# Mamba stages of a fused kernel: one batch and 1024 tokens a step, one scan per 1024 columns, sums over states for two groups at once

## The chip, the cores and the metric

The kernel runs on one core of one Trainium2 chip. The metric is the device time of one execution in microseconds, as the median of several runs; lower is better. The engines are TensorE (PE, matmuls; PEld is its weight load), VectorE (DVE), ScalarE (ACT), GpSimd (POOL) and SyncE (SP, which here issues the DMAs). All run their own instructions in order and wait for each other by semaphores.

## What is computed

Four layers in a row on an image batch of 4 x 96 channels x 64 x 64: a Mamba fusion block, an SSD block, a second Mamba fusion block and a ConvNeXt block. The change touches the two fusion blocks alone, which are the same code with other weights. All is float32. With L = 64 x 64 = 4096 tokens, DIN = 192 inner channels and 16 states per channel, one fusion is, cut to what matters:

```python
seq = x.reshape(b, c, L).transpose(0, 2, 1)
for i in range(2):                                   # two Mamba layers
    h = layernorm(seq); xs, z = split(h @ in_w, 2)
    xc = silu(causal_conv(xs, 4 taps) + conv_b)
    dt, Bm, Cm = split(xc @ xproj_w)                 # 6, 16, 16 columns
    delta = softplus(dt @ dt_w + dt_b)
    dA  = exp(delta[..., None] * A)                  # (b, L, 192, 16)
    dBx = delta[..., None] * Bm[:, :, None, :] * xc[..., None]
    hstates = linear recurrence over L: h[t] = dA[t] * h[t-1] + dBx[t]
    y = einsum('blds,bls->bld', hstates, Cm) + Dp * xc
    seq = seq + (y * silu(z)) @ out_w
gp = relu(x.mean((2, 3)) @ gp_w.T + gp_b)            # pooled branch, per batch
out = fus_w @ concat([mamba_out, broadcast(gp)])     # then batch norm, + x
```

The costly part is the recurrence: 4 batches x 4096 tokens x 192 channels x 16 states, twice per fusion, four times in the kernel.

## The kernel before

**Tiling.** `mamba_fusion` handles the batches in two pairs. `X` (L560) holds both batches of a pair in on-chip memory, channels on partitions. A *step* is one pair, one layer (`sub`) and T = 512 tokens; there are 2 x 2 x 8 = 32 steps per fusion (L623), 64 in the kernel. The 192 channels of two batches make 384 rows, that is three tiles j = 0, 1, 2 of 128 partitions; `SEGS` and `ROWS` (L49 to L55) say which rows of a tile are which channels of which batch: tile 0 is batch 0, tile 2 is batch 1, tile 1 is 64 rows of each.

**Groups.** For the recurrence each partition holds one channel and one state: 8 channels x 16 states fill 128 partitions. A *group* is two such sets (GS = 2), 128 partitions x 2 x 512 columns. A step has 24 groups: j (3) by q (4 blocks of 8 channels in a block of 32) by half p (2), counted in this order. The two sets of a group are quarters p and p + 2 of a tile, so they are different channels, and for j = 1 of different batches; hence they have different decay factors, and for j = 1 different rows of B and C (`b_or_c`, L328).

**One step's front.** `mamba_front` (L159) makes what the groups of a step need: layer norm (L174 to L196), four convolution taps as matmuls into `pu` (L205), silu, the gate rows `pz` (L215), the B, C and step-size rows `pd` (L228), softplus (L283 to L299), then `delta` and `delta * xc` (L251, L252) which are stored to DRAM (L246). B and C rows are stored and read back broadcast (L262). It is a generator: each `next` issues one piece. `PACE` (L279) says how many pieces are issued in each of the 24 iterations, so the front of the next step lies between the groups of this one.

**The run loop** (`Scan.run`, L458) has one iteration per group. In iteration n it issues, in this order: `load` for group n+5 (two DMAs that read 8 rows of delta and broadcast them to 16 states); `spread` for n+1 (TensorE copies delta * xc to the states, L343, into one of two `bs` buffers; for one group in four, the *dma* groups, the spread comes by DMA and `bs` holds the decays instead); `decay` for n+2 (ScalarE exponentials, L357); `after` for n-1 (GpSimd multiplies the scanned states with C into one of four `hc` buffers, L383; ScalarE copies the last column to `carry`, L386); `product` for n+2 (GpSimd, dma groups, L351); `scan` for n (VectorE: product with B, L369, if not a dma group; the gate product `close` of an earlier j, L410; then two scans of 512 columns, L376); the copies of finished output (`keep`, `spread_out`, `reload`); pieces of the front; `sums` for n-3 (TensorE sums over the states into `py`, L402, and adds D * xc, L396); and the output projection (L418 to L426) into `po`. A dependency written out by hand (L497 to L502) keeps this order on every engine. So the order of issue is also the order in which each engine works; an instruction that waits holds back all behind it on its engine.

**Around it.** Before the loop, front(0) runs by itself, and between its pieces the sums of `x` over all tokens for the pooled branch are made (L636 to L647): batches 0 and 1 from `X`, batches 2 and 3 from eight extra loads. `other_weights` (L650) loads the second layer's weights and folds the fusion matrix into them within the first steps. After the last group, statistics for the batch norm are put together (L687).

The two scans of a group are:

```python
for i in range(GS):
    n = NQU * g["quarters"][i] + g["q"]
    init = 0.0 if c == 0 else self.carry[:, j, n : n + 1]
    nc.vector.tensor_tensor_scan(hs[:, i], da[:, i], dbx[:, i], init, ALU.mult, ALU.add)
```

## Time and profile before

| what | value |
|---|---|
| median of the 3 runs | 9624.49 us (9616.18 to 9635.07) |
| span of the profiled execution | 9613.6 us |
| mean granted TensorE clock | 0.938 of full speed |
| busy share PE / DVE / ACT / POOL | 86% / 84% / 58% / 71% |
| scans L376, all forms | 3072 of 128x512 |
| products with C on POOL, L383 | 1536 of 128x1024, mean 2358 ns |
| sums on PE, L402 | 6144 records of 128x512 with 32 columns, mean 633 ns |
| spreads on PE, L343 | 4608 records, mean 682 ns |
| decays on ACT, L111 | 2304 + 768 of 128x512, means 710 and 688 ns |
| first fusion, SSD, second fusion, ConvNeXt begin at | 0, 2969, about 6069 and 9028 us |

How to read it: the profile lists instructions by source line, engine and operation, with the shape of the output and the inputs, the count, the busy time, the mean duration of one, and the idle time of the engine right before it with what ended it. A float32 matmul is recorded as two instructions. Records of neighbouring instructions on one engine can overlap by some tens of nanoseconds, so distances between starts say more than durations. In the timeline each line has start, duration, engine, source line, operation, tiles and a count where several of a kind follow each other. A bracket gives the idle time before and its releaser.

### The profile page before, as it was taken

How to read it: one execution, taken by the hardware profiler on the slowest of the kernel's cores; microseconds unless marked ns; L12 is line 12 of the kernel's file. 1: busy time of each engine (PE TensorE's matmuls, PEld its weight loads, DVE VectorE, ACT ScalarE, POOL GpSimd, SP SyncE). 2: the span in 40 equal slices, each digit the busy share in tenths (PEclk: the TensorE clock that was granted, in tenths of full speed). 3: DMA queues.
4: the chain of work that ended last, by engine and by line, in shares of the span. 5: the costliest groups of instructions: out<-in, count | busy, mean ns of one | idle time of the engine just before them, and what ended most of it. 6: DMA issues, size and time to landing. Idle time of an engine off the chain costs nothing. (4 is left out here: it accounts for less than half of the span.)

```text
span 9613.6 us, 109902 instructions
## 1 busy us (share of the span) xinstructions
PE 8280.0 (86%) x32896; PEld 3476.0 (36%) x32896; DVE 8048.5 (84%) x10870; ACT 5532.2 (58%) x10786; POOL 6872.2 (71%) x4573
## 2 busy tenths in 40 slices
PE   8888888888887998988898899788888888888678
PEld 2222222222213676776776767222222222222122
DVE  8999999999995666666767667799999999999887
ACT  5666666666664455445545544566666666666345
POOL 7888888888884555555555555688888988888511
PEclk8999999999997999999999999899999999999889
DMA  8788888777884223222322322687888877887643
GB/s 214 194 209 214 207 219 211 203 208 205 213 217 117 69 73 90 73 68 81 89 64 77 88 68 63 161 206 198 213 215 213 222 207 199 214 216 205 172 115 84
DMA packets 813856, 1531.93 MB, mean 159 GB/s; under 512 B 126894, under 2 KB 132426, under 8 KB 809803
## 3 DMA queue, kind: packets, MB, share of 16 engines
q1 hardware_dynamic: 810186, 1519.79, 60.5%
q8 instruction: 260, 4.26, 0.2%
q10 hardware_dynamic: 3072, 5.11, 0.1%
q14 instruction: 338, 2.76, 0.1%
HBM read 1229.28 MB, written 148.50 MB: 143 GB/s over the span
## 5 line engine op out<-in xcount | busy, mean ns | idle before, releaser
L383 POOL TENSOR_TENSOR hc<-hs,bc 128x1024 f32<-128x1024 f32 x1536 | 3613.9, 2358 | 671.8 <-DVE hs L376 427.8
L376 DVE TENSOR_TENSOR_SCAN hs<-da,carry,bs 128x512 f32<-128x512 f32 x2016 | 2468.7, 1266 | 98.9 <-ACT bs L111 2.0
L343 PE MATMUL bs<-du,seldu 64*128 64x512 f32 x4608 | 1488.7, 682 | 683.3 <-DVE hs L376 676.8
L402 PE MATMUL py<-hc,selsum 128*32 128x512 f32 x6144 | 1619.3, 633 | 34.4 <-DVE xz L410 28.9
L111 ACT ACTIVATE da<-da,w_a 128x512 f32<-128x512 f32 x2304 | 1518.3, 710 | 9.4 <-DMA da<-dd 9.2
L369 DVE TENSOR_TENSOR bs<-bs,bc 128x1024 f32<-128x1024 f32 x1152 | 1396.9, 1213 | 47.8 <-PE bs L343 37.3
L343 PEld LDWEIGHTS bs<-du,seldu 64*128 64x128 f32 x4608 | 409.0, 196 | 1687.9 <-DVE hs L376 1272.5
L351 POOL TENSOR_TENSOR du<-du,bc 128x1024 f32<-128x1024 f32 x384 | 905.5, 2358 | 17.9 <-DMA du<-dg 9.5
L111 ACT ACTIVATE bs<-da,w_a 128x512 f32<-128x512 f32 x768 | 528.6, 688 | 670.9 <-DVE hs L376 657.3
L1055 DVE TENSOR_SCALAR seg<-dr,dac 128x128 f32<-128x128 f32 x1536 | 636.5, 448 | 281.3 <-PE y L1100 278.7
L1071 POOL TENSOR_TENSOR seg<-seg,cb 128x384 f32<-128x384 f32 x512 | 515.2, 1008 | 480.9 <-DVE cb L1070 405.0
L376 DVE TENSOR_TENSOR_SCAN hs<-bs,carry,du 128x512 f32<-128x512 f32 x672 | 818.8, 1259 | 0.0
L205 PE MATMUL pu<-h,w_conv 96*128 96x512 f32 (+3 forms) x2048 | 794.2, 622 | 1.4 <-POOL h L179 1.4
L1006 PE MATMUL front<-pk,sconv 128*128 128x512 f32 x1536 | 755.2, 609 | 26.7 <-ACT z L994 21.6
L1110 POOL TENSOR_TENSOR y<-y,xs 128x192 f32<-128x192 f32 x496 | 295.9, 597 | 598.0 <-DVE y L1109 581.9
L1123 ACT ACTIVATE y<-yz 128x192 f32<-128x192 f32 x512 | 186.1, 364 | 901.7 <-DVE yz L1122 900.9
L402 PEld LDWEIGHTS py<-hc,selsum 128*32 128x32 f32 x6144 | 217.8, 110 | 1252.5 <-issue 781.2
L1075 POOL TENSOR_TENSOR xs<-pre,coef 128x576 f32<-128x576 f32 x512 | 599.0, 1175 | 51.8 <-ACT pre L116 25.1
L1017 PE MATMUL front<-sconv,pk 128*128 128x192 f32 x3072 | 571.8, 329 | 56.1 <-DVE pre L1022 50.8
L386 ACT COPY carry<-hs 128x2 f32<-128x2 f32 x1344 | 246.8, 184 | 530.6 <-DVE hs L376 530.1
L1017 PEld LDWEIGHTS front<-sconv,pk 128*128 128x128 f32 x3072 | 496.3, 190 | 88.4 <-DVE pre L1022 77.4
L1100 PEld LDWEIGHTS y<-xs,seg 128*128 128x128 f32 x3072 | 440.2, 205 | 141.4 <-issue 80.9
(229 smaller groups left out, 13717.5 us busy)
## 6 DMA issues: line engine op xcount, KB each, us to landing
da<-dd SPq DMA_DIRECT2D x3072, 256.0 KB
du<-dg SPq DMA_DIRECT2D x768, 256.0 KB
dr<-rows SPq DMA_DIRECT2D x256, 384.0 KB
bc<-rows SPq DMA_DIRECT2D x256, 256.0 KB
dd<-delta SPq DMA_DIRECT2D x192, 256.0 KB
dg<-du SPq DMA_DIRECT2D x192, 256.0 KB
pk<-xn SPq DMA_DIRECT2D x128, 384.0 KB
pk<-xn SPq DMA_DIRECT2D x128, 256.0 KB
```

The costliest lines, as they stand in the source:

```text
L111: self.last = self.scalar.activation(out, in_, func, **kw)
L205: nc.tensor.matmul(pu[r0:r1], lhsT=wt["conv"][:kk, tap, d0:d1], rhs=h[:kk, b, ds(tap, T)], start=(tap == 0), stop=(tap == 3),)
L343: nc.tensor.matmul(g["bs"][:, i], lhsT=self.sel["du"][rows, g["half"], g["q"]], rhs=g["made"]["du"][rows, g["j"]], start=True, stop=True,)
L351: self.tc.nc.gpsimd.tensor_tensor(g["du"], g["du"], self.b_or_c(g, 0), ALU.mult)
L369: nc.vector.tensor_tensor(dbx, dbx, self.b_or_c(g, 0), ALU.mult)
L376: nc.vector.tensor_tensor_scan(hs[:, i], da[:, i], dbx[:, i], init, ALU.mult, ALU.add)
L383: nc.gpsimd.tensor_tensor(g["hc"], hs, self.b_or_c(g, 1), ALU.mult)
L402: nc.tensor.matmul(py[rows], lhsT=self.sel["sum"][:, g["q"]], rhs=g["hc"][:, i], start=(g["q"] == 0), stop=(g["q"] == NQU - 1),)
L1006: nc.tensor.matmul(p, lhsT=self.conv[:, i, DI + q * DST : DI + (q + 1) * DST], rhs=pk[:, i, ds(c * T, T)], start=(i == 0), stop=(i == 2),)
L1017: nc.tensor.matmul(p, lhsT=pk[:, i, ds(c * Q, Q)], rhs=self.conv[:, i, :DI], start=(i == 0), stop=(i == 2),)
L1055: nc.vector.tensor_scalar(seg[:, h], g["pair"]["dr"][:, c % 2 * NH + h], made["dac"][:, n0 + h : n0 + h + 1], 0.0, ALU.subtract, ALU.min,)
L1075: nc.gpsimd.tensor_tensor(xs, x.to_broadcast([P, 3, NH, HD]), coef.to_broadcast([P, 3, NH, HD]), ALU.mult)
```

## The change

A step is now one batch, one layer and 1024 tokens (`STEP`). There are again 32 steps per fusion. The lower 64 partitions of every tile hold the first 512 tokens, the upper 64 the next 512, for the same 64 channels (`D0`: tile 0 has channels 0 to 63, tile 1 128 to 191, tile 2 64 to 127). So:

- The two sets of a group are the same 8 channels at neighbouring stretches of time. One scan of 1024 columns goes through both, with one start value and one carry column; one exponential of 1024 columns makes their decays, since the factor is the same; B and C are one plain tile for each group.
- In the front, every matmul over channels becomes two with 64 columns each (one per half of the tokens); the B, C and step-size weights stand on both halves of the partitions, and each half of the rows is multiplied by itself.
- `sums` is called for every second group and issues the four matmuls of two groups (halves p = 0 and 1, which go to four blocks of 32 rows of `py`) behind each other, at lag 3 and 4. The D product comes in the same call.
- The output projection of both token halves follows the last gate of the step (`completed`, lags 4 to 9) instead of one batch after j = 1 and one after j = 2; each has four matmuls. `PACE` is changed, with two iterations without a piece of the front.
- The sums of `x` for the pooled branch are made by ScalarE in the front of layer 0 (a copy with an accumulated sum); the extra loads and reductions before the loop go. The pooled branch is computed per batch (`pooled_rows`), the second layer's weights later, in `later`, a list of generators with starting iterations.
- At the start only batch 0 is loaded; batch 1 follows behind front(0).
- A step with c = 0 starts its scans from 0.0: one step in 4 instead of one in 8.

The core of the diff:

```diff
-SEGS = (
-    ((0, 128, 0, 128, 0),),
-    ((0, 64, 128, 192, 0), (64, 128, 0, 64, 1)),
-    ((0, 128, 64, 192, 1),),
-)
-ROWS = (((0, 0, 128), (1, 0, 64)), ((1, 64, 128), (2, 0, 128)))
+STEP = 2 * T
+NS = L // STEP
+D0 = (0, 128, 64)
...
+            xs = X[:, at, ds(c * STEP + n * T, T)]
             pc = bank("pc")[:C]
-            nc.tensor.matmul(
-                pc, lhsT=k.center, rhs=X[:, n, ds(c * T, T)], start=True, stop=True
-            )
+            nc.tensor.matmul(pc, lhsT=k.center, rhs=xs, start=True, stop=True)
             sq = work.tile([P, T], F32, tag="ua", name="sq", bufs=2)[:C]
+            if parts is not None:
+                nc.scalar.activation(sq, xs, AF.Copy, accum_out=parts[:, 2 * c + n : 2 * c + n + 1])
             nc.scalar.activation(sq, pc, AF.Square)
...
-            for r0, r1, d0, d1, b in SEGS[j]:
+            for i in range(2):
                 nc.tensor.matmul(
-                    pu[r0:r1], lhsT=wt["conv"][:kk, tap, d0:d1], rhs=h[:kk, b, ds(tap, T)],
-                    start=(tap == 0), stop=(tap == 3),
+                    pu[HALFP * i : HALFP * (i + 1)],
+                    lhsT=wt["conv"][:kk, tap, D0[j] : D0[j] + HALFP],
+                    rhs=h[:kk, ds(i * T + tap, T)], start=(tap == 0), stop=(tap == 3),
...
-    for n in range(2):
-        for b in range(2):
-            j, r0, r1 = ROWS[b][n if b == 0 else 1 - n]
+    for j in range(3):
+        for i in range(2):
+            half = ds(HALFP * i, HALFP)
             nc.tensor.matmul(
-                pd[2 * QUART * b : 2 * QUART * (b + 1)], lhsT=wt["xproj"][r0:r1, j],
-                rhs=xz[r0:r1, j], start=(n == 0), stop=(n == 1),
+                pd[half], lhsT=wt["xproj"][half, j], rhs=xz[half, j], start=(j == 0), stop=(j == 2),
...
-PACE = (1,) * 6 + (2, 2, 1, 1) + (2, 1) * 3 + (1,) * 8
+PACE = (1,) * 6 + (2, 0, 2, 2, 0, 2, 2, 2, 1, 1, 1, 2) + (1,) * 6
...
-        if g["j"] == 1:
-            return bc[:, :, which]
-        return bc[:, g["j"] // 2, which : which + 1].to_broadcast([P, GS, T])
+        return g["made"]["bc"][:, which]
...
-        for i in range(GS):
-            n = NQU * g["quarters"][i] + g["q"]
-            self.k.act.exp_ln(
-                out[:, i], g["da"][:, i], AF.Exp, scale=g["wt"]["a"][:, g["j"], n : n + 1]
-            )
+        n = g["n"]
+        self.k.act.exp_ln(out, g["da"], AF.Exp, scale=g["wt"]["a"][:, g["j"], n : n + 1])
...
-        for i in range(GS):
-            n = NQU * g["quarters"][i] + g["q"]
-            init = 0.0 if c == 0 else self.carry[:, j, n : n + 1]
-            nc.vector.tensor_tensor_scan(hs[:, i], da[:, i], dbx[:, i], init, ALU.mult, ALU.add)
+        n = g["n"]
+        init = 0.0 if c == 0 else self.carry[:, j, n : n + 1]
+        out, da, dbx = (x.rearrange("p i t -> p (i t)") for x in (hs, da, dbx))
+        nc.vector.tensor_tensor_scan(out, da, dbx, init, ALU.mult, ALU.add)
...
-        if g["c"] < NT - 1:
-            n = NQU * g["quarters"][0] + g["q"]
-            nc.scalar.copy(self.carry[:, g["j"], n : n + 2 * NQU + 1 : 2 * NQU], hs[:, :, T - 1])
-    def sums(self, g):
+        if g["c"] < NS - 1:
+            n = g["n"]
+            nc.scalar.copy(self.carry[:, g["j"], n : n + 1], hs[:, 1, T - 1 : T])
+    def sums(self, g, other):
         nc = self.tc.nc
-        if g["first"]:
-            g["made"]["py"] = self.psum.tile([P, T], F32, tag="py", name="py", bufs=1)
-        py = g["made"]["py"]
-        if g["q"] == NQU - 1 and g["half"] == 0:
-            nc.tensor.matmul(
-                py, lhsT=g["wt"]["d"][:, g["j"]], rhs=g["made"]["xz"][:, g["j"]], start=False,
-                stop=False,
-            )
-        for i in range(GS):
-            rows = ds(QUART * g["quarters"][i], QUART)
-            nc.tensor.matmul(
-                py[rows], lhsT=self.sel["sum"][:, g["q"]], rhs=g["hc"][:, i],
-                start=(g["q"] == 0), stop=(g["q"] == NQU - 1),
-            )
+        q, j, made = g["q"], g["j"], g["made"]
+        if q == 0:
+            made["py"] = self.psum.tile([P, T], F32, tag="py", name="py", bufs=1)
+        py = made["py"]
+        if q == NQU - 1:
+            nc.tensor.matmul(py, lhsT=g["wt"]["d"][:, j], rhs=made["xz"][:, j], start=False, stop=False)
+        for x in (other, g):
+            for i in range(GS):
+                nc.tensor.matmul(
+                    py[ds(HALFP * i + QUART * x["half"], QUART)], lhsT=self.sel["sum"][:, q],
+                    rhs=x["hc"][:, i], start=(q == 0), stop=(q == NQU - 1),
...
+    def project(self, g, i, part):
         nc = self.tc.nc
-        xz, wt = g["made"]["xz"], g["wt"]
-        po = self.po = self.psum.tile([P, T], F32, tag="po", name="po", bufs=1)[:C]
-        xs = self.X[:, b, ds(g["c"] * T, T)]
-        nc.tensor.matmul(po, lhsT=wt["of_x"], rhs=xs, start=True, stop=False)
-        j, r0, r1 = ROWS[b][0]
-        nc.tensor.matmul(
-            po, lhsT=wt["out"][r0:r1, j], rhs=xz[r0:r1, j], start=False, stop=False
-        )
-    def project_rest(self, g, b):
-        j, r0, r1 = ROWS[b][1]
-        self.tc.nc.tensor.matmul(
-            self.po, lhsT=g["wt"]["out"][r0:r1, j], rhs=g["made"]["xz"][r0:r1, j], start=False,
-            stop=True,
-        )
-    def keep(self, g, b):
-        xs = self.X[:, b, ds(g["c"] * T, T)]
+        if part == 0:
+            self.po = self.psum.tile([P, T], F32, tag="po", name="po", bufs=1)[:C]
+            nc.tensor.matmul(
+                self.po, lhsT=g["wt"]["of_x"], rhs=self.tokens(g, i), start=True, stop=False
+            )
+        half = ds(HALFP * i, HALFP)
+        for j in (2,) if part else (0, 1):
+            nc.tensor.matmul(
+                self.po, lhsT=g["wt"]["out"][half, j], rhs=g["made"]["xz"][half, j], start=False,
+                stop=(j == 2),
+            )
...
+                b=b, sub=sub, c=c, wt=wts[sub], made=made[n], j=j, q=q, half=p, n=NQU * p + q,
+                last=(q == NQU - 1 and p == 1), dma=(q % 2 == 0 and p == 1),
+            )
+            for n, (b, sub, c) in enumerate(steps) for j, q, p in units
...
+            completed(
+                (6, self.keep, 0, (0, 1)), (7, self.spread_out, 0, (1,)), (8, self.reload, 0, (1,)),
+                (9, self.keep, 1, (0, 1)), (10, self.spread_out, 1, (1,)), (11, self.reload, 1, (1,)),
...
-            if n in range(each, each + 14) or n in range(2 * each + 8, 2 * each + 12):
-                next(later, None)
-            if g := at(3):
-                self.sums(g)
-            completed((5, self.project, (0, 1)), (6, self.project_rest, (0, 1)))
+            if later and n >= later[0][0]:
+                if next(later[0][1], True):
+                    later.pop(0)
+            if (g := at(3)) and g["half"]:
+                self.sums(g, at(4))
+            completed(
+                (4, self.project, 0, (0, 1), 0), (5, self.project, 0, (0, 1), 1),
+                (7, self.project, 1, (0, 1), 0), (8, self.project, 1, (0, 1), 1),
...
-    carry = one.tile([P, 3, P // HEIGHT], F32, name="carry")
-    steps = [(pair, sub, c) for pair in range(B // 2) for sub in range(2) for c in range(NT)]
+    carry = one.tile([P, 3, HALFP // HEIGHT], F32, name="carry")
+    steps = [(b, sub, c) for b in range(B) for sub in range(2) for c in range(NS)]
+    parts = one.tile([C, B, NT], F32, name="parts")
...
-    for n, _ in enumerate(front(0, made)):
-        if n in (7, 11):
-            b = n // 4 - 1
-            nc.vector.reduce_sum(gsum[:, b : b + 1], X[:, b], axis=AX.X)
-        if n in (13, 15, 17, 19):
-            for m in range(n - 13, n - 11):
-                b, c = 2 + m // (L // BLK), m % (L // BLK)
-                x = state.tile([P, GS, T], F32, tag="da", name="x", bufs=8)[:C]
-                nc.sync.dma_start(
-                    x, src[b, :, ds(c * BLK, BLK)].rearrange("c (i t) -> c i t", i=GS)
-                )
-                nc.vector.reduce_sum(parts[:, b, c : c + 1], x.rearrange("c i t -> c (i t)"), axis=AX.X)
-    nc.vector.reduce_sum(gsum[:, 2:], parts[:, 2:], axis=AX.X)
-    gb = one.tile([C, B], F32, name="gb")
+    for _ in front(0, made):
+        pass
+    nc.sync.dma_start(X[:, 1], src[1])
...
+    def pooled_rows(b):
+        at = slice(b, b + 1)
+        nc.vector.reduce_sum(gsum[:, at], parts[:, b], axis=AX.X)
+        yield
+        pg = psum.tile([P, T], F32, tag="po", name="pg", bufs=1)[:C, :1]
+        nc.tensor.matmul(pg, lhsT=gpw, rhs=gsum[:, at], start=True, stop=True)
+        nc.scalar.activation(gp[:, at], pg, AF.Relu, bias=vec[:, 0:1], scale=1.0 / L)
+        yield
+        pg = psum.tile([P, T], F32, tag="po", name="pg", bufs=1)[:C, :1]
+        nc.tensor.matmul(pg, lhsT=fus[:, 1], rhs=gp[:, at], start=True, stop=True)
+        nc.scalar.activation(gb[:, at], pg, AF.Identity, bias=vec[:, 1:2])
+    each = 3 * HALFP // HEIGHT
+    later = [(each, other_weights()), (2 * each + 9, folded())] + [
+        ((2 * b * NS + NS - 1) * each + 9, pooled_rows(b)) for b in range(B)
```

## The prediction

> **What bounds the kernel now.** I read the shares by slice first, then the two Mamba stages apart from the rest, then VectorE's groups, its waits, and stretches of the timeline.

> ```profile
> DVE  8999999999995666666767667799999999999887
> POOL 7888888888884555555555555688888988888511
> DMA  8788888777884223222322322687888877887643
> ```

> VectorE is full in slices 1 to 12 and 26 to 37 and in no others: these are the two Mamba fusions, the only code that the change touches. SSD and ConvNeXt between and behind them stay as they are. A steady window inside the first fusion (us, then the busy time of PE, PEld, DVE, ACT, POOL, the granted clock, the DMA share and GB/s):

> ```profile
> 600.00:2700.00 2100.00, 1828.89 (x5791) 434.57 (x5788) 1972.99 (x1787) 1335.70 (x2484) 1830.23 (x881) 0.95 0.81 210
> ```

> VectorE is busy for 94% of it, TensorE and GpSimd for 87%, ScalarE for 64%, the DMA engines for 81%. So VectorE sets the pace, with two engines close behind. 557 of the 1536 groups (a group is one pass of the run loop, 1024 columns) lie in this window, 3.77 us each; a step of 24 groups takes 90.5 us, the window is 23.2 steps, and the kernel has 64 of them. VectorE's main groups in the window and everything that it waited for by name:

> ```profile
> L376 DVE TENSOR_TENSOR_SCAN hs<-da,carry,bs 128x512 f32<-128x512 f32 x726 | 889.0, 1266 | 35.2 <-ACT bs L111 0.5
> L369 DVE TENSOR_TENSOR bs<-bs,bc 128x1024 f32<-128x1024 f32 x417 | 506.0, 1213 | 11.4 <-PE bs L343 6.9
> L376 DVE TENSOR_TENSOR_SCAN hs<-da,bs 128x512 f32<-128x512 f32 x108 | 125.8, 1206 | 5.5 <-ACT bs L111 0.5
> L410 DVE TENSOR_TENSOR xz<-py,xz 128x512 f32<-128x512 f32 x69 | 47.4, 687 | 66.6 <-PE py L402 66.6
> ```

> The reader is to see that the scans are over 60% of VectorE's time, and that its one real wait is the gate product at L410 for TensorE's sums: 66.6 us, with 6.9 us at L369 makes 73.5 us, or 3.2 us a step.

> **Scans, two of 512 columns into one of 1024.** Mean durations overlap, so I price by distances between starts.

> ```profile
> 1590.65 1.21 DVE L369 TENSOR_TENSOR bs<-bs,bc 128x1024 f32<-128x1024 f32 x1
> 1591.76 0.68 DVE L410 TENSOR_TENSOR xz<-py,xz 128x512 f32<-128x512 f32 x1
> 1592.36 2.32 DVE L376 TENSOR_TENSOR_SCAN hs<-da,bs 128x512 f32<-128x512 f32 x2
> ...
> 1598.18 2.31 DVE L376 TENSOR_TENSOR_SCAN hs<-bs,du 128x512 f32<-128x512 f32 x2
> 1600.41 1.21 DVE L369 TENSOR_TENSOR bs<-bs,bc 128x1024 f32<-128x1024 f32 x1
> 1601.72 2.33 DVE L376 TENSOR_TENSOR_SCAN hs<-da,bs 128x512 f32<-128x512 f32 x2
> 1603.97 1.21 DVE L369 TENSOR_TENSOR bs<-bs,bc 128x1024 f32<-128x1024 f32 x1
> ...
> 1611.27 0.66 DVE L178 TENSOR_TENSOR h<-pc,rs 96x512 f32<-96x512 f32 x1
> 1611.85 2.44 DVE L376 TENSOR_TENSOR_SCAN hs<-bs,carry,du 128x512 f32<-128x512 f32 x2
> ...
> 1624.54 2.45 DVE L376 TENSOR_TENSOR_SCAN hs<-da,carry,bs 128x512 f32<-128x512 f32 x2
> 1626.90 2.43 DVE L376 TENSOR_TENSOR_SCAN hs<-bs,carry,du 128x512 f32<-128x512 f32 x2
> ```

> A pair of scans that start from the carry takes 2.36 us (1624.54 to 1626.90), a pair that starts from zero 2.25 (1601.72 to 1603.97): reading the carry costs 0.055 a scan. No row has a scan of 1024 columns. The nearest are products: one of 1024 takes 1.11 (1590.65 to 1591.76), one of 512 takes 0.60 (L410) or 0.58 (L178), so a merge of two saves 2 x 0.58 - 1.11 = 0.05 to 2 x 0.60 - 1.11 = 0.09 us. I take 0.06, near the lower end, since the 0.58 has the same plain 512 columns and no accumulated sums to read; with the second carry read 0.115. Bounds for a merged scan that starts from the carry: 0 (the scan's cost is all per column) and 0.09 + 0.055 = 0.145. As a step is now a quarter of one batch, one group in 4 starts from zero instead of one in 8. A group's scans before: 7/8 x 2.36 + 1/8 x 2.25 = 2.346 us; after: 3/4 x 2.245 + 1/4 x 2.19 = 2.231. That is 0.115 x 24 = 2.76 us a step, **177 us** over 64. With the upper bound it is 0.145 x 24 x 64 = 223, and with the lower only the extra starts from zero, 1/8 x 0.11 x 1536 = 21.

> [...]

> **Sums over states, two groups at once (TensorE).** 48 products a step of 128 rows by 32 columns remain, but four column groups now stand next to each other. The trace has this case already, where two iterations happened to meet:

> ```profile
> 1518.48 1.06 PE L402 MATMUL py<-hc,selsum 128*32 128x512 f32 x8
> ...
> 1628.98 1.08 PE L205 MATMUL pu<-h,w_conv 96*64 96x512 f32 x4
> 1629.98 1.05 PE L402 MATMUL py<-hc,selsum 128*32 128x512 f32 x4
> ...
> 1632.00 1.13 PE L343 MATMUL bs<-du,seldu 64*128 64x512 f32 x4
> 1633.06 1.94 PE L205 MATMUL pu<-h,w_conv 96*64 96x512 f32 x8
> ```

> (Each matmul is recorded twice, so x8 is four.) Eight take 1.06 us, four take 1.05: 12 x 1.0 = 12 us less TensorE a step.

> **The front (TensorE).** The convolution has 24 matmuls instead of 16, all of 64 columns in pairs; a pair takes what a 128-column one does (x4 1.08), so it stays at 12 x 0.95. The same holds for the gate rows (4 to 6) and the step-size rows (4 to 6). The B/C rows go from 2 pairs to 3, +0.9 us. The output projection takes 8 single matmuls instead of 6, +2 us. Net about 9 us a step less.

> But TensorE is late in one stretch, and there the change adds. Take the 8 iterations from the first convolution tap on. Before: 12 taps 11.4, 6 spreads of 1.06 6.4, 8 sums 7.8, the D product 0.95, half the output projection 3.1, together 29.7 us; VectorE needs 6 x 3.70 + 2 x 2.36 + 0.6 = 27.5. After: 11.4 + 6.4 + 4 sums of 1.0 + 0.95 + both halves of the projection 2 x 3.9 = 30.6, against 6 x 3.585 + 2 x 2.245 + 0.6 = 26.6. The excess grows from 2.2 to 4.0 us. TensorE runs its instructions in order, so behind each late sum stands the spread for the next L369, and VectorE stands behind that. Some of this is absorbed by the two bs buffers. I followed the stretch iteration by iteration with these durations (a spread starts when the scan two groups back has ended; its product needs it one scan later; the gate needs the sums of the iteration before). For the code before, this gave 2.4 us of VectorE stall a step where the profile has 3.2; for the code after 2.95, at the gate of j=2 (0.2), at two spreads (0.6, 0.95) and at the gate of j=0 (1.2). I take the difference, +0.5 us a step, **+35 us**. Bounds: all waits go (-3.2 a step, -205 us), or the added excess is not absorbed at all (+1.8, +115 us).

> [...]

> **ScalarE.** 24 decays of 1024 columns replace 48 of 512. One of 512 takes 710 ns; the silu of 1536 takes 1483 and an exponential of 512 with a fixed scale 630, so 0.83 ns a column, and one of 1024 takes 710 + 427 = 1137 ns: 6.8 us a step less. Carry copies (184 ns) fall from 1344 to 1152. Added are two row sums of X in half the steps, about 0.6 + 0.19 us each. ScalarE is busy 64% and waited 670.9 us for scans, so neither counts. Without that cover they'd be worth 1% at most.

> **GpSimd and queues.** GpSimd's work is the same: 24 + 6 products of 2.358, six of 1.27, two of 0.77: 79.9 us a step. SP issues as many loads and stores a step as before; four more small weight loads per layer (0.3 to 0.6 us of SP each) fall into the start, behind which SP issues 16 loads of w_a for 11.8 us, or into the first step. The eight loads and ten reductions for the pooled mean go (18 us of VectorE a fusion), but the first softplus at 46.54 us waited only about 0.3 us for them, so I count nothing.

> **Tail.** Before, only the second batch was projected behind the last gate: 3.2 to 5.7 us from its end to the statistics. Now also the first half's last matmul (1.0), its copy (0.7) and the second's three first matmuls (2.9): about **+5 us** a fusion, 10 in all.

> **Sum.** Against the profiled execution: 9613.6 - 177 + 35 + 10 = 9481.6 us of span. The median of the runs is 9624.49, 10.9 more than this span, so 9492.5; I say **9492**.

> **Rivals.**
> (1) *The waits on TensorE go.* Net 9 us less work a step may let it catch up before the gate of j=0. For it: the whole of it waits for scans for 233 us in the window. Against: the lateness comes from one stretch, which gets fuller. With half the 3.2 us gone instead of 0.5 added: 9492 - 64 x 2.1 = 9358; with all gone 9252.
> (2) *The four product buffers make GpSimd the bound (slower).* hc has four buffers; group m reuses that of m-4. Before, its sums were issued two iterations ahead of that reuse, now for every even group only one, and in the iterations with convolution taps they come last. GpSimd then waits, and scans stop when their own four buffers are full. For it: GpSimd already waits for TensorE at L383 in the window (49.7 + 34.8 + 9.3 us, 4 us a step). Against: such a wait arises only where TensorE is late, five even iterations of twelve by my walk, 5.6 us in all, and 79.9 + 5.6 is below 87.7. It decides from 10.6 us a step on (90.5 - 79.9). If every pair waits 1.2 us, as at the first, it is 79.9 + 14.4 = 94.3 us a step, 64 x 3.8 = 243 slower: 9867; with 1.0 us 91.9, 9714.
> (3) *The merged scan saves nothing.* Then only the starts from zero help: 9624 - 21 + 10 + 35 = 9648, or without the added stall 9613. The 0.05 at least of the products speaks against.
> (4) *Transfers.* The DMA share would rise from 0.81 to 0.84; ScalarE waited 9.4 us for them in the whole run. I give this nothing of its own.

> **Chances.** Forecast 0.60, rival 1 0.14, rival 2 0.16, rival 3 0.10. A difference of 0.2%, 19 us, is about what this kernel's runs can tell from none. Faster by more: 0.75 (the forecast and rival 1, and a little of 3); within: 0.07; slower: 0.18. The likeliest case has its own range from 9410 (upper bound of the scans, stall +0.2) to 9570 (excess not absorbed). For 8 in 10: from 9350, about half of rival 1, to 9650, rival 3.

> **What would show it.** Scans: 1536 records of 128x1024 at 2.27 (from zero) to 2.34 us (carry); over 2.40, the first step is wrong. L402: runs of x8 at 1.05 to 1.10; at 2 us the sums aren't side by side. VectorE's waits for TensorE at the gate and at the product: 3.0 to 4.5 us a step; under 2 is rival 1. GpSimd's waits for TensorE above 10 us a step are rival 2. The last gate to the statistics: about 10 us. The prediction is wrong if a step in the same stretch isn't between 86.5 and 89.5 us.

## The result and the profile after

The kernel after takes **9883.74 us** (9880.49 to 9884.79, four runs) beside 9624.31 (9616.18 to 9635.07) for the kernel before: a ratio of 1.027, interval 1.0255 to 1.0284. It is slower by 259 us where 132 less were forecast. The profiled execution has a span of 9881.9 us (9613.6 before) and a mean granted clock of 0.884 (0.938). Its shares by slice, on the page of the kernel after:

```profile
DVE  6898888888886666666666667688888888888887
PEclk8888888888887999999999999888888888888789
```

VectorE isn't full any longer: it stood at 9 in slices 2 to 12 and 27 to 37, which lie in the two fusions, and is at 8 in all of them but one. TensorE's granted clock is lower exactly there, 8 for 9; in the SSD block (slices 14 to 25), whose code is the same, it stays at 9. The same window as before, in the same columns (PE, PEld, DVE, ACT, POOL busy, clock, DMA share, GB/s):

```profile
600.00:2700.00 2100.00, 1721.11 (x6286) 421.09 (x6284) 1844.88 (x1194) 1180.03 (x1830) 1753.71 (x849) 0.86 0.78 202
```

Every engine is busy for less of it than before: VectorE 88% instead of 94%, TensorE 82 instead of 87, GpSimd 84 instead of 87, at a clock of 0.86 instead of 0.95. Nothing has become a full engine; all wait for each other. 534 groups lie in the window, 22.25 steps of 94.4 us (before 90.5). For one step, VectorE is busy for 1844.88 / 22.25 = 82.9 us (before 85.0) and stands still for 255.1 / 22.25 = 11.5 (before 5.5). So 2.1 us of the 2.76 of the merged scans came, and 6.0 us of new waits took their place: 64 x (6.0 - 2.1) = 250, all but 9 of the 259. VectorE's scans and the two groups that wait most, in the window of the kernel after:

```profile
L372 DVE TENSOR_TENSOR_SCAN hs<-da,carry,bs 128x1024 f32<-128x1024 f32 x312 | 731.6, 2345 | 91.5 <-ACT carry L382 37.6 <-issue 11.5 <-ACT means L611 10.2
L365 DVE TENSOR_TENSOR bs<-bs,bc 128x1024 f32<-128x1024 f32 x401 | 486.1, 1212 | 24.6 <-PE bs L342 24.4
L372 DVE TENSOR_TENSOR_SCAN hs<-da,bs 128x1024 f32<-128x1024 f32 x90 | 205.6, 2285 | 27.1 <-ACT carry L382 16.9 <-issue 4.3 <-ACT bs L110 1.9
L404 DVE TENSOR_TENSOR xz<-py,xz 128x512 f32<-128x512 f32 x67 | 46.2, 690 | 83.5 <-PE py L396 82.8
```

What VectorE waited for by name in that window (total us, times, longest):

```profile
DVE xz L404 <- PE py L396: 82.8, 44, 4.6
DVE hs L372 <- ACT carry L382: 54.5, 18, 3.4
DVE bs L365 <- PE bs L342: 24.4, 37, 2.3
DVE hs L372 <- POOL du L350: 19.7, 19, 1.5
...
DVE hs L372 <- ACT da L110: 11.1, 5, 3.4
DVE hs L372 <- ACT means L611: 10.2, 3, 3.4
```

The gate (L404) waits 3.7 us a step for TensorE, 2.9 before; the product (L365) 1.1, 0.3 before. New are the scans: the rows for `carry`, `da` and `means` make 75.8 us, 3.4 a step, where before there were none of these. `carry` and `means` are only what ScalarE happened to work on; what is late is the decay that the scan reads, as the timeline below shows. And 0.9 a step for GpSimd's product `du`. Together 0.8 + 0.8 + 3.4 + 0.9 = 5.9 of the 6.0 us. (The short named waits of the scans, under 0.6 us each, are 1.3 us a step more, and VectorE's idle time without a name is as much less.) GpSimd and ScalarE in the same window:

```profile
POOL hc L379 <- PE py L396: 243.8, 102, 5.5
POOL hc L379 <- DVE hs L372: 83.7, 22, 3.8
```

```profile
ACT xz L211 <- PE po L420: 236.9, 22, 10.9
```

GpSimd waits 11.0 us a step for the sums over the states (4 before). ScalarE's copy L211 waits for the output projection once in a step, 10.8 us each time (6.0 before).

Three causes can be read from the trace; the experiments test them. **A, a buffer of the step before.** One stretch of the kernel after (start, duration, engine, line, operation; in brackets the idle time before it and its releaser):

```profile
1515.49 1.10 PE L420 MATMUL po<-xz,w_out 64*96 64x512 f32 x2
1516.62 0.59 ACT L211 COPY xz<-pu 128x512 f32<-128x512 f32 x1 [10.67 <-PE po L420]
1517.10 1.15 ACT L110 ACTIVATE da<-da,w_a 128x1024 f32<-128x1024 f32 x1
1518.34 2.35 DVE L372 TENSOR_TENSOR_SCAN hs<-da,carry,bs 128x1024 f32<-128x1024 f32 x1 [3.38 <-ACT means L611]
1520.60 2.33 DVE L372 TENSOR_TENSOR_SCAN hs<-bs,carry,du 128x1024 f32<-128x1024 f32 x1
1522.84 1.21 DVE L365 TENSOR_TENSOR bs<-bs,bc 128x1024 f32<-128x1024 f32 x1
```

L211 is the first copy of the next step's front. It writes `xz`, of which there are two; the one it gets belonged to the step before the current one, and that step's output projection still reads it: its last matmuls, now issued four iterations after the step's last gate (two before the change), end at 1516.59. ScalarE works in order, so the decay behind the copy starts at 1517.10, and VectorE stands for 3.38 us. **B, the product buffers**: rival 2 of the prediction, GpSimd's 11.0 us. **C, TensorE after standing still.** A stretch of the same trace, some 20 us earlier:

```profile
1487.09 1.98 PE L342 MATMUL bs<-du,seldu 64*128 64x512 f32 x4 [2.45 <-DVE hs L372]
...
1489.84 2.08 PE L342 MATMUL bs<-du,seldu 64*128 64x512 f32 x4 [0.76 <-DVE hs L372]
...
1491.84 3.37 PE L205 MATMUL pu<-h,w_conv 96*64 96x512 f32 x8
...
1496.20 1.06 PE L396 MATMUL py<-hc,selsum 128*32 128x512 f32 x8
1497.20 1.13 PE L342 MATMUL bs<-du,seldu 64*128 64x512 f32 x4
1497.36 0.69 DVE L404 TENSOR_TENSOR xz<-py,xz 128x512 f32<-128x512 f32 x1 [2.30 <-PE py L396]
```

After 2.45 us without work the spreads take 1.98 and 2.08 us instead of 1.13, the taps 3.37 instead of 1.94 (the same x8 at 1501.17), and the gate stands 2.30 us for the sums behind them. The trace's own record of the clock says why (stretch, us, then busy time of PE, PEld, DVE, ACT, POOL, the granted clock, DMA share, GB/s):

```profile
1480.40:1483.82 3.42, 3.42 (x19) 0.86 (x22) 2.88 (x3) 1.47 (x4) 2.13 (x1) 1.00 0.72 170
1483.82:1487.23 3.41, 0.96 (x10) 0.17 (x4) 3.22 (x3) 3.38 (x6) 3.41 (x3) 1.00 0.55 154
1487.23:1490.64 3.41, 2.65 (x6) 0.77 (x8) 3.41 (x4) 2.11 (x3) 3.41 (x3) 0.50 0.63 173
1490.64:1494.06 3.42, 3.42 (x9) 1.07 (x7) 3.33 (x3) 0.00 (x0) 3.42 (x3) 0.50 1.05 255
1494.06:1497.47 3.41, 3.41 (x17) 0.87 (x15) 1.11 (x2) 0.00 (x0) 0.84 (x2) 1.00 0.78 188
```

The clock is at full speed through the pause, falls to half just as work comes back, and stays there for 6.8 us, into the stretch in which TensorE is late. Over the window a spread's mean duration is 782 ns, 681 before.

### The profile page after: what moved, and what is told of

The parts are those of the page before. It is cut to its first block, busy times and chain, and to the rows that moved or that the text cites. A ratio compares the mean times of both kernels' runs of the same rounds, so it can differ in the third digit from the quotient of the medians.

```text
span 9881.9 us, 114335 instructions
## 1 busy us (share of the span) xinstructions
PE 8204.4 (83%) x34968; PEld 3499.3 (35%) x34968; DVE 7872.1 (80%) x9328; ACT 5221.0 (53%) x9190; POOL 6849.2 (69%) x4573
## 5 line engine op out<-in xcount | busy, mean ns | idle before, releaser
L342 PE MATMUL bs<-du,seldu 64*128 64x512 f32 x4608 | 1732.6, 783 | 1005.2 <-DVE hs L372 950.1
L372 DVE TENSOR_TENSOR_SCAN hs<-da,carry,bs 128x1024 f32<-128x1024 f32 x864 | 2026.0, 2345 | 250.0 <-ACT carry L382 106.5
L365 DVE TENSOR_TENSOR bs<-bs,bc 128x1024 f32<-128x1024 f32 x1152 | 1396.4, 1212 | 82.7 <-PE bs L342 81.5
L110 ACT ACTIVATE da<-da,w_a 128x1024 f32<-128x1024 f32 x1152 | 1302.1, 1139 | 9.0 <-DMA da<-dd 9.0
L342 PEld LDWEIGHTS bs<-du,seldu 64*128 64x128 f32 x4608 | 468.7, 220 | 2093.0 <-issue 1413.3
L396 PE MATMUL py<-hc,selsum 128*32 128x512 f32 x6144 | 890.8, 653 | 9.5 <-POOL hc L379 7.6
L205 PE MATMUL pu<-h,w_conv 96*64 96x512 f32 (+1 forms) x3072 | 850.9, 668 | 43.1 <-ACT xz L211 40.5
L110 ACT ACTIVATE bs<-da,w_a 128x1024 f32<-128x1024 f32 x384 | 426.6, 1111 | 706.5 <-DVE hs L372 385.1
L372 DVE TENSOR_TENSOR_SCAN hs<-da,bs 128x1024 f32<-128x1024 f32 x288 | 658.0, 2285 | 79.0 <-ACT carry L382 47.4
L372 DVE TENSOR_TENSOR_SCAN hs<-bs,carry,du 128x1024 f32<-128x1024 f32 x288 | 671.9, 2333 | 38.7 <-POOL du L350 35.4
L1111 PE MATMUL y<-xs,seg 128*128 128x64 f32 x3072 | 445.9, 281 | 29.5 <-POOL seg L1082 25.4
```

The lines of the kernel that those rows point to most:

```text
L110: self.last = self.scalar.activation(out, in_, func, **kw)
L205: nc.tensor.matmul(pu[HALFP * i : HALFP * (i + 1)], lhsT=wt["conv"][:kk, tap, D0[j] : D0[j] + HALFP], rhs=h[:kk, ds(i * T + tap, T)], star ...
L342: nc.tensor.matmul(g["bs"][:, i], lhsT=self.sel["du"][rows, g["half"], g["q"]], rhs=g["made"]["du"][rows, g["j"]], start=True, stop=True,)
L365: nc.vector.tensor_tensor(dbx, dbx, self.b_or_c(g, 0), ALU.mult)
L372: nc.vector.tensor_tensor_scan(out, da, dbx, init, ALU.mult, ALU.add)
L396: nc.tensor.matmul(py[ds(HALFP * i + QUART * x["half"], QUART)], lhsT=self.sel["sum"][:, q], rhs=x["hc"][:, i], start=(q == 0), stop=(q == ...
```

## The experiments

All are the kernel after with the edit shown; below, A, B and C in the expectations are the three causes. Ratios are to the kernel before, measured beside each, with their intervals; differences between runs are taken from the ratios, times 9630.

| run | time, us | ratio to before |
|---|---|---|
| (after) | 9883.7 | 1.027 (1.0255 to 1.0284) |
| xz3 | 9799.5 | 1.0173 (1.0156 to 1.019) |
| hc6 | 9781.7 | 1.0156 (1.0136 to 1.0176) |
| xz3_hc6 | 9743.2 | 1.0112 (1.0092 to 1.0132) |
| fill_pe | 9760.8 | 1.013 (1.0115 to 1.0146) |
| all3 | 9663.9 | 1.0035 (1.0024 to 1.0047) |
| sums1 | 9923.3 | 1.0308 (1.0291 to 1.0325) |
| sums1_xz3_hc6 | 9830.7 | 1.021 (1.0195 to 1.0225) |
| fill_more | 9993.2 | 1.0376 (1.0361 to 1.0392) |
| all3_fill_pd | 9569.0 | 0.9944 (0.9925 to 0.9962) |
| paced | 9503.9 | 0.9865 (0.9851 to 0.988) |
| paced_scan512 | 9742.4 | 1.0105 (1.0088 to 1.0123) |
| paced_hc4 | 9671.3 | 1.0033 (1.0021 to 1.0046) |

### One cause at a time

**xz3**: a third `xz`, so that the copy needn't wait for the projection.

```diff
-    xz = made["xz"] = work.tile([P, 6, T], F32, name="xz", bufs=2)
+    xz = made["xz"] = work.tile([P, 6, T], F32, name="xz", bufs=3)
```

> The changed kernel with three xz buffers instead of two; all else stays. Theory A (ScalarE held up): the copy xz<-pu of the next step writes the xz buffer of the step before, whose second output projection now ends four iterations later; ScalarE stands there for 10.7 us a step, the decays behind it are late, and VectorE waits for them 3.4 us a step (75.8 us of the 2100 us window, 22.2 steps). A expects that ScalarE's wait at the copy falls below 2 us a step, VectorE's waits for decays vanish, and the time falls by about 64 x 3.4 = 218 us, to 9620 to 9720. Theory B (four hc buffers make GpSimd wait for the sums, 11 us a step) expects 9860 to 9900: the stall only moves to another wait. Theory C (TensorE's granted clock, 0.86 against 0.95, makes the stretch with the convolution slow) expects under 60 us, 9830 to 9884.

**hc6**: six product buffers instead of four.

```diff
-        g["hc"] = self.state.tile([P, GS, T], F32, name="hc", bufs=4)
+        g["hc"] = self.state.tile([P, GS, T], F32, name="hc", bufs=6)
```

> The changed kernel with six hc buffers instead of four. Theory B: GpSimd's wait for the sums falls from 11 us a step to under 3, and the time to 9500 to 9650. Theory A: GpSimd waits because scans and sums are late, not the other way round; its wait is renamed (for scans), the time stays within 50 us, 9830 to 9890. Theory C: as A.

Waits of VectorE and GpSimd in the window, first xz3, then hc6:

```profile
DVE xz L404 <- PE py L396: 108.3, 45, 4.9
DVE bs L365 <- PE bs L342: 41.9, 63, 1.1
...
POOL hc L379 <- PE py L396: 314.0, 127, 5.6
```

```profile
DVE xz L404 <- PE py L396: 66.7, 45, 3.9
DVE hs L372 <- ACT carry L382: 54.1, 16, 3.4
...
POOL hc L379 <- PE py L396: 41.9, 34, 1.3
```

In xz3 the copy's wait for `po` and the scans' waits for ScalarE are gone, so the mechanism of A is shown; but only 93 us came back, less than half of what A expected, since GpSimd's wait grew from 243.8 to 314.0 and the gate's from 82.8 to 108.3. In hc6 GpSimd's wait falls to 41.9 and the scans' wait for ScalarE stays: B is a cause by itself, worth 110 us, and not the whole. It had reached VectorE by GpSimd's product `du` (19.7 us of waits, now 1.1) and by the gate (82.8, now 66.7). Neither time lies in a range that was expected of it: no cause alone makes the 259 us, and each removed wait uncovers another.

**xz3_hc6**: both. Only the planes of `xz` that the projection reads get a third buffer; the gate rows become a tile `z` of their own.

```diff
-    xz = made["xz"] = work.tile([P, 6, T], F32, name="xz", bufs=2)
+    xz = made["xz"] = work.tile([P, 3, T], F32, name="xz", bufs=3)
+    z = made["z"] = work.tile([P, 3, T], F32, name="z", bufs=2)
...
-        g["hc"] = self.state.tile([P, GS, T], F32, name="hc", bufs=4)
+        g["hc"] = self.state.tile([P, GS, T], F32, name="hc", bufs=6)
```

> The changed kernel with the gate rows in a tile of their own (two buffers), xz of three tiles with three buffers, and six hc buffers. If A holds alone: the time of xz3 within 40 us. If A and B both hold: at least 80 us below the better of xz3 and hc6, 9450 to 9560. If only C holds: above 9800.

It brings 152 us, less than 93 + 110, and misses the 9450 to 9560 expected of A and B together. What remains is TensorE (waits of VectorE):

```profile
DVE xz L405 <- PE py L397: 100.0, 46, 4.4
DVE bs L366 <- PE bs L343: 50.3, 86, 1.1
```

### TensorE's clock

**fill_pe**: the kernel after, with two needless matmuls in each of the last two layer-norm pieces, four a step, where TensorE stood still before the convolution. Nobody reads what they write.

```diff
+        if n >= 4:
+            fill = psum.tile([P, T], F32, tag="po", name="fill", bufs=1)[:C]
+            for _ in range(2):
+                nc.tensor.matmul(fill, lhsT=k.mean, rhs=centered[0][1], start=True, stop=True)
```

> The changed kernel with four needless matmuls of 96x96 by 512 a step (two in each of the two iterations ahead of the convolution, where TensorE stands still for 2 to 3 us and the next spreads and taps take twice as long). Theory C: the granted clock in the window rises from 0.86 to 0.90 or more, the first spreads and taps fall from 2.0 and 3.4 us to 1.1 and 1.9, and the time falls by 60 to 200 us although TensorE has 4 us more work a step. A and B: no gain, 9870 to 9950.

**all3**: xz3_hc6 with these four.

> xz of three buffers, six hc buffers and the four needless matmuls ahead of the convolution, together. If the three causes are separate, their gains add: 9743 (the two buffers together) less 123 (the matmuls alone) is 9620, say 9590 to 9660, that is no difference from the kernel before to 0.5% slower. If the matmuls only hide the same wait as the buffers: above 9700.

The window of fill_pe, and the gate's wait in it:

```profile
600.00:2700.00 2100.00, 1773.23 (x6616) 440.95 (x6614) 1885.32 (x1219) 1198.86 (x1860) 1793.55 (x868) 0.91 0.79 207
```

```profile
DVE xz L408 <- PE py L400: 39.5, 45, 2.1
```

More work on TensorE makes the kernel 135 us faster: the clock rises from 0.86 to 0.91, a record of a spread falls from 782 to 723 ns and one of a tap from 687 to 610, and the gate's wait halves. That is hard to explain by anything but C, as no buffer and no order of the needed work is changed. all3 stands 74 us below xz3_hc6, just outside the range for gains that add, and is the first to come near the kernel before.

**all3_fill_pd**: all3 with three more needless matmuls behind the last gate rows, ahead of the B, C and step-size rows, where another slow stretch was left (twelve records of `pd` took 4.49 us in one step of xz3, and 2.79 in one of xz3_hc6; in all3's window one takes 872 ns on average).

```diff
+        if j == 2:
+            fill = psum.tile([P, T], F32, tag="po", name="fill", bufs=1)[:C]
+            for _ in range(3):
+                nc.tensor.matmul(fill, lhsT=k.mean, rhs=h[:C, ds(3, T)], start=True, stop=True)
```

> all3 with three more needless matmuls behind the last gate row, where TensorE otherwise stands still for 2.8 us before the B/C rows and then needs 4.5 us for them instead of 2.8, and VectorE waits 2.2 us for the next spread. C (slow after standing still, and it costs only where VectorE waits behind it): the B/C rows fall to 3 us, the wait at the product after them goes, and the time falls by 60 to 140 us, 9520 to 9600. If TensorE's amount of work is what counts: slower than all3, above 9664.

Another 88 us. The mean granted clock of the profiled execution rises from all3's 0.903 to 0.920, a record of `pd` falls from 872 to 598 ns, and VectorE's wait at the product from 69.9 to 34.7 us: with seven needless matmuls a step the changed kernel is faster than the one before.

**fill_more**: all3 with two there, and three in each of two softplus pieces:

```diff
+        if n in (3, 4):
+            fill = psum.tile([P, T], F32, tag="po", name="fill", bufs=1)[:C]
+            for _ in range(3):
+                nc.tensor.matmul(fill, lhsT=k.mean, rhs=h[:C, ds(3, T)], start=True, stop=True)
```

> all3 with eight more needless matmuls a step, two ahead of the B/C rows and six behind the softplus, where TensorE also stands still for 2.4 to 4.4 us and is slow afterwards. C in general (the clock is lost wherever TensorE stands still): granted clock 0.93 or more in the window, 20 to 60 us below all3. C only ahead of the convolution: within 25 us of all3.

It missed: 328 us slower than all3, where 20 to 60 less or no change were expected. The fills in the softplus pieces write the same accumulator bank (`po`) as a tile of softplus, and so wait until VectorE has read it and hold up everything behind them on TensorE:

```profile
PE fill L287 <- DVE lg L314: 73.8, 22, 3.8
```

The clock is at 0.92 in the window and the kernel slower all the same, so the run doesn't say what the clock is worth there; it shows again what instructions that wait (73.8 us in the window) do to all that is issued behind them on their engine.

### The sums of two groups at once, undone

**sums1**: the kernel after, but each group's sums are issued at lag 3 by themselves, two column groups side by side as before the change.

```diff
-        for x in (other, g):
+        for x in (g,):
...
-            if (g := at(3)) and g["half"]:
-                self.sums(g, at(4))
+            if g := at(3):
+                self.sums(g)
```

> The changed kernel with the sums issued for each group by itself at lag 3, two products side by side, as before the change (12 us more TensorE time a step); all else as changed. If the sums of two groups at once cost through B (later release of hc) and C (a TensorE that stands still), this brings the granted clock to 0.91 or more, GpSimd's wait for the sums under 5 us a step, and the time to 9660 to 9780 although TensorE has more to do. If the change's own idea holds (TensorE's time is what counts), it is slower than the changed kernel: above 9884.

**sums1_xz3_hc6**: the same with the two buffer changes.

> The same with xz of three buffers, the gate rows in a tile of their own, and six hc buffers. If B is served by the sums of one group, hc6 adds nothing and only A is gained: 80 to 100 below sums1, 9570 to 9690. If sums of two groups at once are worth having once the buffers are there, it is slower than the two buffers alone: above 9743.

In both, the second of the two expected cases came true: slower. The window of sums1, and the waits in it of VectorE, ScalarE and GpSimd:

```profile
600.00:2700.00 2100.00, 1800.43 (x6234) 415.06 (x6232) 1832.78 (x1182) 1170.28 (x1815) 1744.10 (x842) 0.95 0.76 200
```

```profile
DVE bs L365 <- PE bs L342: 80.1, 122, 2.0
...
POOL hc L379 <- PE py L396: 24.6, 26, 2.0
```

```profile
ACT xz L211 <- PE po L420: 279.9, 22, 12.8
```

The clock is back at 0.95, GpSimd's wait for the sums is nearly gone, and the gate's falls from 82.8 to 39.7 us. But the sums take the time again that the pairing had saved, and the kernel is 37 us slower than after (94 slower than xz3_hc6 with the buffers): the product now waits for its spread (80.1 for 24.4), and the projection, later still, holds the copy for 12.7 us a step. So the lower clock is a price of the paired sums, but not a reason against them: the work they save is worth more than the clock they cost.

### The front spread differently

**paced**: xz3_hc6 with another `PACE`, no needless work. The same 29 pieces of the front are issued, nine instead of six of them in the first six iterations, and the pauses and doubled pieces of the convolution, the gate rows and the B/C rows lie elsewhere.

```diff
-PACE = (1,) * 6 + (2, 0, 2, 2, 0, 2, 2, 2, 1, 1, 1, 2) + (1,) * 6
+PACE = (2, 1, 1, 2, 2, 1, 1, 0, 2, 1, 0, 2, 2, 1, 1, 2, 1, 1) + (1,) * 6
```

> The two buffers (xz of three, six hc) without needless matmuls, and another PACE: the layer norm is issued two iterations earlier, so the convolution begins in the iterations where TensorE stood still, with at most one tap in the iterations that also have a gate's sums, none beside the projection's first part, and the B/C rows in an iteration without a spread. If the loss is TensorE being idle, hence slow, ahead of an overfull stretch, useful work moved there does what the needless matmuls did: 9480 to 9600, below the kernel before. If it was the needless work's side effect or the order of sums: within 40 of the two buffers alone, 9700 to 9780.

The window of paced, and its waits:

```profile
600.00:2700.00 2100.00, 1791.31 (x6770) 435.47 (x6769) 1977.00 (x1277) 1271.01 (x1959) 1880.77 (x908) 0.89 0.82 216
```

```profile
DVE bs L366 <- PE bs L343: 46.2, 53, 3.3
DVE xz L405 <- PE py L397: 18.1, 45, 0.6
```

**9503.9 us**, a ratio of 0.9865: it beats both kernels, and is 238 us below xz3_hc6. VectorE is busy 94% again. 573 groups in the window are 23.9 steps of 88.0 us, inside the 86.5 to 89.5 that the prediction asked of a step. The gate's wait falls from 100.0 to 18.1 us, and a `pd` record takes 598 ns instead of 746. But the mean clock in the window is only 0.89, as in all3, which is 164 us slower, and it still falls to half 73 times there, where xz3_hc6 has 80 falls. So a higher clock is not the main part of this gain; where the slow matmuls stand and how much work lies beside the gates both change with the edit, and the run doesn't part them. Whether the kernel before would gain from another `PACE` too wasn't tried.

**paced_scan512**: paced with each scan cut in two of 512 columns, the second starting from the last column of the first.

```diff
-        out, da, dbx = (x.rearrange("p i t -> p (i t)") for x in (hs, da, dbx))
-        nc.vector.tensor_tensor_scan(out, da, dbx, init, ALU.mult, ALU.add)
+        for i in range(GS):
+            nc.vector.tensor_tensor_scan(hs[:, i], da[:, i], dbx[:, i], init, ALU.mult, ALU.add)
+            init = hs[:, 0, T - 1 : T]
```

> The paced kernel with each scan of 1024 columns split into two of 512 again, the second starting from the last column of the first. If the merged scan is worth what the prediction gave it (0.06 to 0.115 us a group, and the second scan now always reads a start value and waits for the first, up to 0.1 more), and VectorE sets the pace in the paced kernel, it is 120 to 300 us slower than paced: 9620 to 9800. If the merge is not on the path: within 60 us of paced.

**paced_hc4**: paced with four product buffers.

> The paced kernel with four hc buffers instead of six. B as a cause of its own (GpSimd is held by buffers that the sums of two groups release late): GpSimd waits for the sums over 5 us a step again and the time rises by 40 to 120 us, 9540 to 9620. B only where TensorE is late: within 30 us of paced.

A pair of scans in paced_scan512:

```profile
1498.94 1.28 DVE L373 TENSOR_TENSOR_SCAN hs<-da,carry,bs 128x512 f32<-128x512 f32 x1
1500.26 1.28 DVE L373 TENSOR_TENSOR_SCAN hs<-da,hs,bs 128x512 f32<-128x512 f32 x1
1501.45 1.21 DVE L366 TENSOR_TENSOR bs<-bs,bc 128x1024 f32<-128x1024 f32 x1
```

The pair takes 2.51 us from start to start, the merged scan 2.25, and the kernel 231 us longer: once the waits are gone, the scan's length is on the path, though not wholly, as 0.26 us in 1536 groups would make 399. (The pair of the kernel before took 2.36; the 0.15 more comes with the second scan's start from the first one's last column, so 231 is more than the change brings.) Waits in paced_hc4:

```profile
DVE bs L366 <- PE bs L343: 103.1, 52, 4.6
...
POOL hc L380 <- PE py L397: 220.6, 111, 3.4
```

Four buffers cost 162 us here, more than was expected and more than in the kernel after: rival 2's mechanism doesn't need a late gate (18.4 us here, 18.1 in paced). With four buffers and the sums of one group, in sums1, GpSimd waited 24.6; it comes with the sums for two groups at once. Paced with two `xz` buffers wasn't tried, so what that buffer is worth there stays open.

## Why the prediction was wrong

**The scans: right.** Distances in the trace after are 1520.60 to 1522.84 and its like, 2.24 to 2.26 us from the carry (2.245 predicted); records are 2.345 and 2.285. VectorE's busy time fell by 2.1 us a step where 2.76 were counted. Rival 3, that the merge saves nothing, falls with these distances: a pair took 2.36 before. paced_scan512 adds that the length counts in the time.

**ScalarE, "so neither counts": the step that failed first.** The price was right (a decay of 1024 columns took 1139 ns, 1137 predicted), but ScalarE was weighed by its spare time alone. It is also a queue. The change moves the projection that frees `xz` to the end of the step; the copy L211 stands behind it, and all decays behind the copy. The trace of before had this wait already, 137.7 us in the window, with enough room behind it to do no harm; ten microseconds instead of six used up the room. Where the projection moves, the buffer that it frees should have been followed: 3.4 us of VectorE's time a step went there, which the sum had at nothing. Taking the copy's wait away alone gave 93 us.

**TensorE's stall, "+0.5 us a step": mis-sized.** The gate and the product waited 107.2 / 22.25 = 4.82 us a step, 3.17 before: +1.65, not +0.5, near the upper bound of 1.8. The walk took spreads at 1.06 and taps at full speed from rows in which TensorE had been working. The paired sums did what was said (25.4 to 13.9 us a step, 11.5 less where 12 were predicted), but spreads of the same count took 23.4 us a step before and 27.1 after, the taps 12.5 and 13.5, the B/C rows 2.1 and 3.5 for half as many matmuls again, and TensorE's busy time a step fell by 1.4 us (78.8 to 77.4) instead of 9. The rest came back as slow matmuls after pauses, in and around the stretch that the prediction had named as the late one. Rival 1 had it the wrong way round: TensorE had less to do, and was later for that, as fill_pe and sums1 show, where more work brought the clock up (from 0.86 to 0.91 and 0.95) and halved the gate's wait (from 82.8 us to 39.5 and 39.7). The trace of before showed the effect too: a pause of 3.13 us ahead of 1522.67, and 1.96 us for the spread behind it, at a granted clock of 0.54.

**Rival 2 was right in kind.** It was to decide from 10.6 us of GpSimd's waits a step; they are 11.0, in 4.6 places a step where the walk had five. The walk's size for each was wrong: 2.4 us, not 1.1. Its price, 9867, lies near the measured 9884, but partly by chance: hc6 takes that wait away and recovers 110 of 259 us. GpSimd isn't full either: it also stood 3.8 us a step for late scans.

**The tail** was counted as about 10 us from the last gate to the statistics. It is 15.7 in both fusions (3078.18 to 3093.85 in the first), 22 us more in all than before instead of 10, since the clock stood at 0.50 there: six records of the projection's matmuls took 5.43 us, 0.91 each instead of 0.49.

**The sum.** -177 + 35 + 10 was a sum over the engines' work with one of the new waits in it. With what the window shows, times 64, it reads -134 for the scans, +106 for the gate and the product, +22 for the tail, and +218 and +57 for two waits that stood at nothing, the scans' for ScalarE and for GpSimd: +269, beside 259 measured. The causes behind these waits overlap (93, 110 and 135 us alone, 226 in all3), and none comes from the merged scan itself. (The range's lower end, 9410, adds up to 9424 by its own terms; it decides nothing.) paced, with few of these waits left, takes 9504, close to the forecast of 9492; but its front is spread differently, which the forecast didn't have and the kernel before didn't get, so this nearness doesn't prove the sum right.

## What to carry to other kernels

When a change moves a consumer to a later place, list the buffers it frees, who writes each next, and what is queued behind that writer on its engine; spare time of an engine says nothing about that. Take the price of a matmul from rows at the granted clock that it will have, behind the same pause, not from the best rows: four records of a spread took 2.08 us here at 0.50 (at 1489.84) and 1.13 at 1.00 (at 1497.20). When a larger work item replaces two, the buffers and the hand-written pace around it were fitted to the old ones: change these with it, and then judge.

## What the hardware showed that was not expected

Four to seven needless matmuls a step made the kernel faster, by 135 us for four alone and, beside the two buffers, 88 for three more. And a scan of 512 columns whose start value is the last column of the scan right before it starts 1.32 us after that one (1498.94 to 1500.26), where independent ones stood 1.18 apart in the kernel before.
